# One tile for the output projection's two PSUM banks, evicted by one VectorE product, and one more convolution tap on TensorE in eleven warm-up steps

## The chip, the cores and the metric

One core of a Trainium2 chip, one launch, all data in float32. The metric is the device time of one launch in microseconds (us). The engines are TensorE (PE in the profile, with PEld for its weight loads), VectorE (DVE), ScalarE (ACT), GpSimd (POOL) and SyncE (SP, which here only issues DMAs). Matmuls write into PSUM, which has eight banks of 128 partitions by 512 float32; everything else lies in SBUF.

## The reference, cut to what matters

```python
# x: (2, 768, 64, 64).  d_inner 1536, 4 states per channel, 12 heads of 64
x = x + layer0(group_norm(x))
x = x + layer1(group_norm(x))

def layer0(h):                        # selective scan over 4096 positions per image
    x  = h @ in_proj_w.T              # 768 -> 1536 channels
    xs = silu(depthwise_conv3x3(x) + conv_b)
    dt, Bs, Cs = split(xs @ x_proj_w.T, [48, 4, 4])
    delta = softplus(dt @ dt_w.T + dt_b)
    s[t]  = exp(delta * A) * s[t-1] + (delta * xs) * Bs      # 4 states per channel
    y     = sum_over_states(s * Cs) + D * xs
    y     = layer_norm(y) * ln_g + ln_b                      # over the 1536 channels
    return y @ out_proj_w.T           # 1536 -> 768 channels

def layer1(h):                        # attention by channel statistics
    w   = h @ W_qkv.T                 # 768 -> 768
    Pi  = softmax over the heads of sum_d (w / |w|_over_positions)**2 * temp
    dots = sum over positions of Pi_n * w**2
    return -(w * Pi / (1 + dots)) @ W_out.T
```

## The kernel before, in words

**Layer 0** is a pipeline of 192 steps (NQ0): 16 tiles of 512 positions (NI, 8 image rows each, TL = 512), times 12 chunks of 128 channels (KI). The main loop calls `step(g)` for one (tile, chunk) after the other; the order of all instructions in it is written out by hand (`tc.manual_schedule()`), so every engine works its queue in the order of the code. In step g the scan of chunk g runs. Work for later and earlier chunks lies beside it:

- the input projection of chunk n = g + 17 (`in_proj`, matmul L375), whose result ScalarE copies into a padded image `xs`;
- the convolution taps of chunk a = g + AHEAD = g + 15. Nine taps are split: the middle one is ScalarE's (`tap_act`, L438); those in DMA_TAPS are scaled by ScalarE (`taps_act`, L450) and added by accumulating DMAs; those in PE_TAPS are matmuls with a diagonal matrix into the accumulator's bank (`taps_pe`, L477, the diagonal written by ScalarE in `diag`, L432); what is left, three to five, are VectorE's (`taps_dve`, L491), one instruction each. The tables repeat every four chunks;
- for chunk g: POOL's du = delta * u (`du`, L548), VectorE's product with B (`scan`, L567), the scan (L570) and the product with C (`times_c`, L577); POOL's `sum1` (L556) and accumulating DMAs form y; ScalarE's `square` (L587) and TensorE's `sums_pair` (L597) the layer norm's sums;
- the output projection of a tile runs 12 steps behind (BEHIND): in each step `out_proj` (L636) accumulates three chunks into two banks, for two of the six output chunks, kk by kk, bank 0 then bank 1. Every fourth step these two are full.

After the four steps `out_evict` (L650) multiplies the two banks by the row `rs` (the inverse deviation of the layer norm) into two SBUF buffers. It is called in steps g = 16, 20, ..., 204: from `taps_dve`, after the first of VectorE's taps; from step 177 on, where there are no taps any more, at that place in the step, but for 180, 184 and 188, where it comes in the scan of the step before, after L567 (`early`). Then `out_residual` (L658, an accumulating DMA on POOL's queue) adds x, `out_sums` (L672, two steps after the evict) takes the next group norm's sums on ScalarE, and `out_store` (L680, SP's queue) writes the two to DRAM.

SBUF buffers of 512 columns come from one FIFO of N_SLOT slots: `take()` takes the oldest free one, `give()` returns one.

**PSUM**: psA, psC, psX, psS hold one bank each, psZ one tile of two banks, psO two tiles of one bank each, tags po0 and po1. The users of psO are: the output projection (po0 and po1); odd chunks of the input projection in the first steps, and the lower rows of the first tile (po1); Strassen's w (po0) and x (po1) in the second layer; and two of the six tiles in `spread` (ppo). One output group of the last tile uses psZ instead (poz).

**Layer 1** does its two projections mostly in Strassen's form with seven products (`strassen`, matmul L921), each of three matmuls of 256 columns. (The trace counts two instructions for each matmul of the code, here and elsewhere: a product shows as six, often as a row of x4 and one of x2.) A block q of kind "p1" (the first projection) or "p3" (the second, which adds the residual) goes: t1 into w[:, lo], b21 into x[:, lo], ScalarE's copy of w into p5 (L1003), t2 into y, VectorE's addition of y and p5 into x[:, hi] (L1010), the next block's b11 into another bank y2, eviction of x[:, lo] (`evict`: VectorE L946 and ScalarE's squares L947 for p1, one VectorE addition for p3), t3 into y. Then, in a p1 block only, VectorE adds y and p5 (L1019) and ScalarE squares that sum for its accumulated total, with w[:, lo] as the place for the squares, which nobody reads (L1020). Then b22 into x[:, hi], t4 into y, the eviction of x[:, hi], ScalarE's copy of y2 into the next x (L962), and the eviction of y. In the profile the tiles of all blocks appear as po_p (w and x), psa_p and acc_p (y). There are 30 blocks of p1 with L1020 in the page's counts and 42 of p3.

Of the kernel before, what the change touches and what calls it, by code (L numbers as in the profile page):

```python
# [7 lines left out]
F32 = mybir.dt.float32  # L8
# [6 lines left out]
P = 128  # L15
# [7 lines left out]
KI = DI // P  # L23
# [8 lines left out]
TL = TR * W  # L32
NT = H // TR
NI = NB * NT
NQ0 = NI * KI
# [12 lines left out]

DMA_TAPS = ((0, 2, 6), (0, 2, 6), (0, 2, 6), (0, 2))
PE_TAPS = ((), (1,), (), (1, 7))  # L50
FILL_TAPS = ((0, 2), (0, 2, 6))
NA = 5 * W

AHEAD = 15
BEHIND = 12

N_SLOT = AHEAD + BEHIND + 9 + 9 + 1
N_WEIGHT = 4
N_MORE = 33

# [8 lines left out]
def both_layers(  # L69
# [5 lines left out]
    wp = ctx.enter_context(tc.tile_pool(name="l0w", bufs=1))  # L75
# [29 lines left out]
    rs = wp.tile([P, TL], F32, name="rs")  # L105

    slots = [wp.tile([P, TL], F32, name=f"u{j}") for j in range(N_SLOT)]

    def take():
        return slots.pop(0)  # L110

    give = slots.append
# [7 lines left out]
    def give_w(w):  # L120
        wst.append(w.rearrange("p k m -> p (k m)"))
# [5 lines left out]
    psO = ctx.enter_context(tc.tile_pool(name="l0_pso", bufs=1, space=PSUM))  # L127
    psS = ctx.enter_context(tc.tile_pool(name="l0_pss", bufs=1, space=PSUM))


    spare = psC.tile([P, 512], F32, tag="acc", name="acc_spare")

# [179 lines left out]
    xts, wis, wos, pas, accs, dgs, pxs, pzs, sts, pos, xrs = {}, {}, {}, {}, {}, {}, {}, {}, {}, {}, {}  # L312

    def where(n):
        i, c = divmod(n, KI)
        return i, c, i // NT, i % NT
# [43 lines left out]
    def in_proj(n):  # L360
        i, c, b, t = where(n)
        nn = TL if t < NT - 1 or b + 1 < NB else TL - W
        w = wis.pop(n)
        if KI <= n < AHEAD + 2 and n % 2:
            pa = psO.tile([P, 512], F32, tag="po1", name=f"pa{n}")
        else:
            pa = psA.tile([P, 512], F32, tag="psa", name=f"pa{n}")
        parts = [(pa, slice(0, nn))]
        if i == 0:
            pl = psO.tile([P, 512], F32, tag="po1", name=f"pl{n}")  # L370
            parts = [(pa, slice(0, NA)), (pl, slice(NA, TL + W))]
            pas["low", n] = pl
        for o, cols in parts:
            for k in range(KM):
                nc.tensor.matmul(  # L375
                    o[:, : cols.stop - cols.start], w[:, k, :], xts[i, k][:, cols], start=(k == 0), stop=(k == KM - 1)
                )
        pas[n] = pa
        give_w(w)
        if c == KI - 1:  # L380
            for k in range(KM):
                xt = xts.pop((i, k))
                if i:
                    give(xt)
# [23 lines left out]
    def dma_taps(a):  # L408
        return DMA_TAPS[a % 4] if a >= AHEAD else FILL_TAPS[a < 8] if a != KI - 1 else ()

    def pe_taps(a):
        return PE_TAPS[a % 4] if a > AHEAD else ()

# [206 lines left out]
    def out_proj(g, behind_first=lambda: None):  # L622
        i, r = (g - BEHIND) // KI, g % KI
        w = wos.pop(g)
        give_w(w)
        if r % 4 == 0:
            if i == NI - 1 and r == 4:
                pz = psZ.tile([P, 2, 512], F32, tag="pz", name=f"poz_{g}")
                pos[0] = [pz[:, e, :] for e in range(2)]
            else:  # L630
                pos[0] = [psO.tile([P, 512], F32, tag=f"po{e}", name=f"po{e}_{g}") for e in range(2)]
        po = pos[0]
        for kk in range(3):
            k = 3 * (r % 4) + kk
            for e in range(2):
                nc.tensor.matmul(  # L636
                    po[e], w[:, kk, e * P : (e + 1) * P], us[i * KI + k], start=(k == 0), stop=(k == KI - 1)
                )
            if r // 4 == 2:
                give(us.pop(i * KI + k))  # L640
            if kk == 0:
                behind_first()

    def out_evict(g):

        po = pos[0]
        i, r = (g - 1 - BEHIND) // KI, (g - 1) % KI
        for e in range(2):
            xr = take()
            nc.vector.tensor_mul(xr, po[e], rs)  # L650
            xrs[i, 2 * (r // 4) + e] = xr

    def out_residual(g):
# [20 lines left out]
    def out_store(g):  # L674
        i, r = (g - 3 - BEHIND) // KI, (g - 3) % KI
        b, t = divmod(i, NT)
        for e in range(2):
            m = 2 * (r // 4) + e
            xr = xrs.pop((i, m))
            nc.sync.dma_start(x1[b][m * P : (m + 1) * P, t * TL : (t + 1) * TL], xr)  # L680
            give(xr)


    scale1 = [gp.tile([P, KM], F32, name=f"scale1_{b}") for b in range(NB)]
# [4 lines left out]
    x1s, w1s, pis, pits, ats, dots, phs = {}, {}, {}, {}, {}, {}, {}  # L689
# [202 lines left out]
    def strassen(todo, last=(), beside=lambda q, place: None, then=()):  # L892
# [9 lines left out]
        have, xr, at = {}, {}, {"load": 0, "use": 0}  # L902
# [30 lines left out]
        def load_res(q):  # L933
            if q < len(blocks) and blocks[q][0] == "p3":
                _, b, j, m = blocks[q]
                for r in range(2):
                    xr[q, r] = load_xr1(b, j, m + KH * r)
# [14 lines left out]
        def bank(pool, tag, q):  # L952
            return pool.tile([P, 512], F32, tag=tag, name=f"{tag}_{'_'.join(map(str, blocks[q]))}")

        def first(q):
            y = bank(*((psA, "psa"), (psC, "acc"))[q % 2], q)
            times(y[:, lo], "b11", start=True)
            return y

        def copy(q, y):  # L960
            x = bank(psO, "po1", q)
            nc.scalar.copy(x[:, lo], y[:, lo])  # L962
            return x

# [22 lines left out]
        def some_jobs(q):  # L987
            run(scalar_jobs, 2)
            run(pool_jobs, 4 if q % KH == 2 else 2)

        def products():
            y = first(0)
            x = copy(0, y)
            stores = []
            for q, (kind, b, j, m) in enumerate(blocks):
                load_res(q + 1)
                jobs_of(q)
                beside(q, 0)
                w = bank(psO, "po0", q)
                times(w[:, lo], "t1", start=True)  # L1000
                times(x[:, lo], "b21")
                p5 = wk.tile([P, TL], F32, tag="sq", name=f"p5_{'_'.join(map(str, blocks[q]))}", bufs=3)[:, lo]
                nc.scalar.copy(p5, w[:, lo])  # L1003
                if kind == "p3":
                    nc.gpsimd.tensor_add(xr[q, 1][:, hi], p5, xr[q, 1][:, hi])
                some_jobs(q)
                beside(q, 1)
                times(y[:, lo], "t2")
                run(stores)
                nc.vector.tensor_add(x[:, hi], y[:, lo], p5)  # L1010
                y2 = first(q + 1) if q + 1 < len(blocks) else None
                evict(q, x[:, lo], 0, 0)
                beside(q, 2)
                some_jobs(q)
                times(y[:, lo], "t3")
                if kind == "p1":
                    w1s[b, m + KH, j] = take()
                    c22 = w1s[b, m + KH, j][:, hi]
                    nc.vector.tensor_add(c22, y[:, lo], p5)  # L1019
                    nc.scalar.activation(  # L1020
                        w[:, lo], c22, AF.Square, accum_out=ss[b][:, m + KH, 2 * j + 1 : 2 * j + 2]
                    )
                else:
                    evict(q, y[:, lo], 1, 1)
                times(x[:, hi], "b22")
                times(y[:, lo], "t4")
                if m == KH - 1:
                    tile_done(kind, b, j)
                evict(q, x[:, hi], 0, 1)
                if y2 is not None:  # L1030
                    x = copy(q + 1, y2)
                some_jobs(q)
                evict(q, y[:, lo], 1, 0)
                if kind == "p3":
                    stores = [
                        (lambda d, v: lambda: store_out(*d, v))((b, j, m + KH * r), xr.pop((q, r))) for r in range(2)
                    ]
                y = y2
            run(scalar_jobs)
            run(stores)  # L1040
# [70 lines left out]
    def spread(b, j, ms):  # L1111

        for m in ms:
            if m in (0, 4):
                pits["z"] = psZ.tile([P, 2, 512], F32, tag="pz", name=f"ppz{b}_{j}_{m}")
            if m == 2:
                pits["o"] = [psO.tile([P, 512], F32, tag=f"po{e}", name=f"ppo{e}_{b}_{j}") for e in range(2)]
            pb = pits["o"][m % 2] if m in (2, 3) else pits["z"][:, m % 2, :]
            r = 32 * (m % 4)
            nc.tensor.matmul(pb, esel[r : r + HEADS, m, :], pits[b, j][r : r + HEADS, :], start=True, stop=True)  # L1120
            pits[b, j, m] = pb
# [565 lines left out]
```

## Time and profile before

| | |
|---|---|
| median of 3 runs (lowest to highest) | 3651.55 us (3648.76 to 3654.29) |
| the profiled run, its span | 3651.83 us, 3650.0 us |
| granted TensorE clock, mean | 0.991 |
| PE busy, PEld | 3533.1 us (97%), 1785.9 us (49%) |
| DVE, ACT, POOL busy | 2811.2 us (77%), 2573.5 us (71%), 1796.1 us (49%) |
| L636 output projection | 2256 matmuls, 1001.6 us busy |
| L570 scan | 192, 851.1 us, 4433 ns each |
| L491 VectorE taps | 690, 520.0 us, 754 ns each |
| window 170 to 325 us | PE 115.63 of 155.00, DVE 147.90, ACT 128.93, clock 0.86 |
| window 325 to 2450 us | PE 2105.89 of 2125.00, DVE 2053.52, ACT 1892.87, clock 1.00 |
| window 3150 to 3314 us (p1 blocks) | PE 163.40 of 164.00, DVE 38.80, ACT 76.72, clock 1.00 |

A row of a timeline gives the start in us from the begin of the span, the time taken, the engine and line, the operation, tile written <- tiles read with their shapes, xN where N instructions are drawn as one row, and in brackets the idle time of the engine before the row and what ended it. ACTIVATION_READ_ACCUMULATOR is the reading out of ScalarE's running sum. The granted clock says how fast TensorE was let run, 1.00 being full speed.

### The profile page before, as it was taken

The page shows a single profiled execution, that of the slowest core. Times are in us where ns is not written, and L with a number is a line of the kernel's source. Part 1 is how long each engine was busy: PE and PEld are TensorE (multiplying, and loading weights), DVE is VectorE, ACT ScalarE, POOL GpSimd, SP SyncE. Part 2 cuts the span into 40 slices and gives each one's busy share as a digit, 9 for nine tenths or more (in the row PEclk, how much of TensorE's full clock was granted, in tenths as well). Part 3 has the DMA queues.
Part 4 walks back from the last instruction along what each step waited for, and adds up shares of the span by engine and source line. Part 5 has one row for each costly group of instructions (what it writes and reads, how often), then busy time and mean ns, then how long its engine had stood idle before and what let it go on. Part 6 is the DMA issues. An engine that isn't in the chain of part 4 may idle for free. (4 is left out here: it accounts for less than half of the span.)

```text
span 3650.0 us, 37942 instructions
## 1 busy us (share of the span) xinstructions
PE 3533.1 (97%) x11202; PEld 1785.9 (49%) x11202; DVE 2811.2 (77%) x2528; ACT 2573.5 (71%) x5028; POOL 1796.1 (49%) x1808
## 2 busy tenths in 40 slices
PE   6879999999999999999999999999999999999999
PEld 4423444444434444344344444433347658885688
DVE  8899999999999999999999999996722352225522
ACT  2788988988899898988889898886633532244221
POOL 2555656565655666665556665653444213330242
PEclk9989999999999999999999999999999999999999
DMA  9668899998989989899888989986566538863587
GB/s 350 207 133 178 179 215 204 202 210 189 209 185 217 206 192 208 188 214 205 183 197 190 210 189 217 207 188 162 144 199 209 172 109 268 262 204 119 168 268 241
DMA packets 374333, 729.79 MB, mean 200 GB/s; under 512 B 42912, under 2 KB 115200, under 8 KB 370032
## 3 DMA queue, kind: packets, MB, share of 16 engines
q0 software_dynamic: 142176, 262.73, 41.8%
q1 hardware_dynamic: 231952, 464.64, 38.7%
q8 instruction: 90, 1.47, 0.2%
q14 instruction: 115, 0.94, 0.1%
HBM read 439.11 MB, written 60.03 MB: 137 GB/s over the span
## 5 line engine op out<-in xcount | busy, mean ns | idle before, releaser
L636 PE MATMUL po<-u,w 128*128 128x512 f32 x2256 | 1001.6, 592 | 1.8 <-DVE u L650 1.8
L375 PE MATMUL pa<-u,w 128*128 128x512 f32 (+1 forms) x2160 | 966.7, 597 | 1.6 <-ACT carry L400 1.6
L570 DVE TENSOR_TENSOR_SCAN s<-da,s 128x2052 f32<-128x2052 f32 x192 | 851.1, 4433 | 21.0 <-DVE s L567 1.4
L636 PEld LDWEIGHTS po<-u,w 128*128 128x128 f32 x2256 | 428.1, 190 | 539.3 <-issue 528.0
L375 PEld LDWEIGHTS pa<-u,w 128*128 128x128 f32 x2160 | 406.3, 192 | 555.0 <-issue 534.8
L556 POOL TENSOR_TENSOR ysum<-da 128x1024 f32<-128x1024 f32 x192 | 386.2, 2011 | 556.5 <-DVE da L577 486.0
L491 DVE SCALAR_TENSOR_TENSOR acc<-xs,pc,acc 128x512 f32<-128x512 f32 x690 | 520.0, 754 | 27.5 <-ACT acc L438 6.1
L567 DVE TENSOR_TENSOR s<-du,bc 128x2048 f32<-128x2048 f32 x192 | 439.2, 2288 | 81.7 <-POOL du L548 79.5
L456 POOL DMA_DIRECT2D tm<-tm x309 | 268.7, 870 | 455.2 <-ACT tm L450 397.2
L544 ACT ACTIVATE da<-dl,neg_a 128x512 f32<-128x512 f32 x768 | 489.6, 713 | 0.0
L577 DVE TENSOR_TENSOR da<-s,bc 128x2048 f32<-128x2048 f32 x192 | 440.0, 2292 | 6.3
L563 POOL DMA_DIRECT2D u<-ysum x384 | 379.6, 1254 | 3.0 <-issue 1.9
L450 ACT ACTIVATE tm<-xs,pc 128x512 f32<-128x512 f32 x486 | 317.1, 717 | 10.2 <-DMA tm<-tm 5.1
L438 ACT ACTIVATE acc<-xs,pc 128x512 f32<-128x512 f32 x192 | 131.6, 686 | 211.0 <-DVE u L491 200.8
L548 POOL TENSOR_TENSOR du<-dl,u 128x512 f32<-128x512 f32 x192 | 245.2, 1277 | 0.0
L460 POOL DMA_DIRECT2D u<-tm x177 | 209.6, 1184 | 38.0 <-DMA tm<-tm 13.0
L921 PE MATMUL po_p<-u,w 128*128 128x256 f32 x684 | 177.6, 379 | 0.1
L597 PE MATMUL st<-sq,ones 128*32 128x512 f32 x384 | 130.0, 625 | 37.2 <-ACT sq L587 37.0
L921 PE MATMUL po_p<-v,w 128*128 128x256 f32 x612 | 160.2, 379 | 1.5 <-ACT po_p L1020 1.4
L491 DVE SCALAR_TENSOR_TENSOR u<-xs,pc,acc 128x512 f32<-128x512 f32 x192 | 143.6, 748 | 8.3
L477 PE MATMUL acc<-xs,dg 128*128 128x512 f32 x264 | 135.3, 622 | 11.5 <-ACT acc L438 11.4
L560 ACT ACTIVATE u<-u,pc 128x512 f32<-128x512 f32 x192 | 136.7, 712 | 7.1 <-POOL du L548 7.1
(291 smaller groups left out, 5001.5 us busy)
## 6 DMA issues: line engine op xcount, KB each, us to landing
u<-ysum POOLq DMA_DIRECT2D x384, 256.0 KB, 5.9
tm<-tm POOLq DMA_DIRECT2D x309, 256.0 KB, 4.7
w<-in_wP SPq DMA_DIRECT2D x192, 384.0 KB, 4.1
w<-wo_dr SPq DMA_DIRECT2D x192, 384.0 KB, 4.8
u<-x SPq DMA_DIRECT2D x277, 256.0 KB, 4.4
w<-s_dr_p SPq DMA_DIRECT2D x288, 192.0 KB, 2.9
u<-tm POOLq DMA_DIRECT2D x177, 256.0 KB, 6.2
bc<-bc_dr SPq DMA_DIRECT2D x32, 1024.0 KB, 7.9
```

The lines of the kernel that those rows point to most:

```text
L375: nc.tensor.matmul(o[:, : cols.stop - cols.start], w[:, k, :], xts[i, k][:, cols], start=(k == 0), stop=(k == KM - 1))
L450: nc.scalar.activation(tm.rearrange("p (h w) -> p h w", w=W), xs[:, dy : dy + TR, dx : dx + W], AF.Copy, scale=pc[:, c, PC_W + j : PC_W + ...
L456: nc.gpsimd.dma_start(tms[a][0], tms[a][q], accum_op=ALU.add)
L491: nc.vector.scalar_tensor_tensor(dst, xs[:, dy : dy + TR, dx : dx + W], pc[:, c, PC_W + j : PC_W + j + 1], acc, ALU.mult, ALU.add)
L544: nc.scalar.activation(das[g % 2][:, n, 1:], deltas[g], AF.Exp, scale=neg_a[:, c, n : n + 1])
L556: nc.gpsimd.tensor_add(ysum[:, 0 : 2 + g % 2 : 1 + g % 2, :], da[:, 0:2, 1:], da[:, 2:4, 1:])
L563: nc.gpsimd.dma_start(us[g], ysums(g, n), accum_op=ALU.add)
L567: nc.vector.tensor_mul(s[:, :, 1:], dus.pop(g).unsqueeze(1).to_broadcast([P, NS, TL]), bc[:, :NS, :])
L570: nc.vector.tensor_tensor_scan(sf, das[g % 2].rearrange("p n l -> p (n l)"), sf, 0.0, ALU.mult, ALU.add)
L577: nc.vector.tensor_mul(das[g % 2][:, :, 1:], s[:, :, 1:], bc[:, NS:, :])
L636: nc.tensor.matmul(po[e], w[:, kk, e * P : (e + 1) * P], us[i * KI + k], start=(k == 0), stop=(k == KI - 1))
L921: nc.tensor.matmul(dst, half[:, k, :], tiles[blocks[seq[i][0]][:3]][what][k], start=(start and k == 0), stop=(k == KH - 1), skip_group_che ...
```

## The change

Three things. psO holds one tile `po_both` of two banks, made once, and all users of po0 and po1 take its halves by `po_bank(0)` and `po_bank(1)`. In the 41 evictions of steps 16 to 176 (`paired`), one VectorE product of 128x2x512 writes a fixed buffer `xr_both` of two chunks; the residual DMAs, sums and stores work on its halves, and the halves go to the slots with the last such store; in exchange N_SLOT is two less. The other seven evictions stay two products into slots. WARM_TAPS gives tap 1 to TensorE in the even chunks a = 16 to 26 too, which are prepared by steps g = 0 to 10 and would be VectorE's in steps 1 to 11.

```diff
+WARM_TAPS = ((1,), (1,), (1,), (1, 7))
-N_SLOT = AHEAD + BEHIND + 9 + 9 + 1
+N_SLOT = AHEAD + BEHIND + 9 + 9 - 1
...
+    po_both = psO.tile([P, 2, 512], F32, tag="po", name="po")
+    xr_both = wp.tile([P, 2, TL], F32, name="xr")
+
+    def po_bank(e):
+        return po_both[:, e, :]
...
 def in_proj(n):
-            pa = psO.tile([P, 512], F32, tag="po1", name=f"pa{n}")
+            pa = po_bank(1)
...
-            pl = psO.tile([P, 512], F32, tag="po1", name=f"pl{n}")
+            pl = po_bank(1)
...
 def pe_taps(a):
-        return PE_TAPS[a % 4] if a > AHEAD else ()
+        return (PE_TAPS if a > AHEAD + KI else WARM_TAPS)[a % 4] if a > AHEAD else ()
...
 def out_proj(g, ...):
-                pos[0] = [psO.tile([P, 512], F32, tag=f"po{e}", name=f"po{e}_{g}") for e in range(2)]
+                pos[0] = [po_bank(e) for e in range(2)]
...
+    def paired(g):
+        return g < NQ0 - AHEAD
+
     def out_evict(g):
         po = pos[0]
         i, r = (g - 1 - BEHIND) // KI, (g - 1) % KI
+        if paired(g):
+            nc.vector.tensor_mul(xr_both, po_both, rs.unsqueeze(1).to_broadcast([P, 2, TL]))
         for e in range(2):
-            xr = take()
-            nc.vector.tensor_mul(xr, po[e], rs)
+            if paired(g):
+                xr = xr_both[:, e, :]
+            else:
+                xr = take()
+                nc.vector.tensor_mul(xr, po[e], rs)
             xrs[i, 2 * (r // 4) + e] = xr
...
 def out_store(g):
-            give(xr)
+            if not paired(g - 2) or not paired(g + 2):
+                give(xr)
...
 def copy(q, y):
-            x = bank(psO, "po1", q)
+            x = po_bank(1)
...
 def products():
-                w = bank(psO, "po0", q)
+                w = po_bank(0)
...
 def spread(b, j, ms):
-                pits["o"] = [psO.tile([P, 512], F32, tag=f"po{e}", name=f"ppo{e}_{b}_{j}") for e in range(2)]
+                pits["o"] = [po_bank(e) for e in range(2)]
```

## The prediction

> **What bounds the kernel now.** I read the page first, then VectorE's timeline in the front and in the steady stretch, then the timelines of all engines around three uses of the banks that the change joins.
>
> ```profile
> PE 3533.1 (97%) x11202; PEld 1785.9 (49%) x11202; DVE 2811.2 (77%) x2528; ACT 2573.5 (71%) x5028; POOL 1796.1 (49%) x1808
> ```
>
> TensorE is the bound over the whole, and in the second layer it is the only one: the windows give it 163.40 busy us of 164.00 in 3150 to 3314, where VectorE has 38.80. From 170 to 325 it is otherwise: TensorE 115.63 of 155.00 at a granted clock of 0.86, VectorE 147.90. From 325 to 2450 both are near the end, 2105.89 and 2053.52 of 2125.00. VectorE's timeline in the front:
>
> ```profile
> 222.75 4.43 DVE L570 TENSOR_TENSOR_SCAN s<-da,s 128x2052 f32<-128x2052 f32 x1
> ...
> 235.64 4.43 DVE L570 TENSOR_TENSOR_SCAN s<-da,s 128x2052 f32<-128x2052 f32 x1
> ...
> 245.75 2.29 DVE L567 TENSOR_TENSOR s<-du,bc 128x2048 f32<-128x2048 f32 x1 [0.32 <-POOL du L548]
> 248.14 4.43 DVE L570 TENSOR_TENSOR_SCAN s<-da,s 128x2052 f32<-128x2052 f32 x1
> ```
>
> Scan to scan, the step with five VectorE taps takes 12.89 us, the next with four 12.50. The four-tap step has a wait of 0.32 for POOL's du that the five-tap step hides. So a tap less is worth 0.39 there, not its 0.78 (four took 3.12). The output eviction in the steady stretch, VectorE's timeline:
>
> ```profile
> 629.68 1.28 DVE L650 TENSOR_TENSOR u<-po,rs 128x512 f32<-128x512 f32 x2
> 630.88 1.54 DVE L491 SCALAR_TENSOR_TENSOR acc<-xs,pc,acc 128x512 f32<-128x512 f32 x2
> ```
>
> Two products hold VectorE for 1.20 us, start to next start. Now all engines near the end of layer 0, where the products wait for the matmuls. First with po0 and po1 as two tiles:
>
> ```profile
> 2493.62 4.46 PE L636 MATMUL po<-u,w 128*128 128x512 f32 x10
> ...
> 2497.26 0.69 DVE L650 TENSOR_TENSOR u<-po,rs 128x512 f32<-128x512 f32 x1 [2.25 <-PE po L636]
> ...
> 2498.12 0.69 DVE L650 TENSOR_TENSOR u<-po,rs 128x512 f32<-128x512 f32 x1 [0.17 <-PE po L636]
> ```
>
> The first product starts 0.82 before the last matmul ends (2493.62 + 4.46 = 2498.08): it waited for its own bank only. Then a step whose banks are one tile of two (poz, out of psZ):
>
> ```profile
> 2734.55 3.17 PE L636 MATMUL poz<-u,w 128*128 128x512 f32 x7
> ...
> 2737.75 1.29 DVE L650 TENSOR_TENSOR v<-poz,rs 128x512 f32<-128x512 f32 x2 [30.21 <-PE poz L636]
> ```
>
> The matmuls, in the same order of banks, end at 2737.72, and both products start after that, back to back. **A tile of two banks is waited for as a whole.** That is the row on which my forecast turns, because the change puts the Strassen tiles w (po0) and x (po1) into one tile as well. A "p1" block on the timeline:
>
> ```profile
> 3212.32 1.03 PE L921 MATMUL po_p<-u,w 128*128 128x256 f32 x4
> ...
> 3213.04 0.39 ACT L1020 ACTIVATE po_p<-u 128x256 f32<-128x256 f32 x1 [1.64 <-DVE u L1019]
> ...
> 3213.36 0.19 ACT L1020 ACTIVATION_READ_ACCUMULATOR po_p<-u 128x1 f32 x1
> ...
> 3214.85 0.36 ACT L962 COPY po_p<-acc_p 128x256 f32<-128x256 f32 x1
> 3214.91 1.03 PE L921 MATMUL po_p<-u,w 128*128 128x256 f32 x4
> ```
>
> The first row is b22 into x; L1020 writes its unused squares into w, which is then free; L962 copies into the next x while t1, the last row, goes into the next w. Today none of these meets another's bank.
>
> **The change part by part.** All sums stand against the profiled run, 3651.83 (span 3650.0), 0.28 above the median of 3651.55.
>
> *One more TensorE tap in steps 1 to 11.* Six VectorE taps go, at odd steps. The scan periods of steps 1 to 12 alternate 12.89 and 12.50, but for step 2, whose 2.44 wait for POOL's du swallows what step 1 saves: 5 x 0.39 = **-1.95** (six would give -2.3, none 0). Added: 12 tap matmuls (L477) at a pitch of 0.43, 5.2 us in the 39.4 that TensorE idles in that window, and six diag writes on ScalarE (L432), 0.4 each, in its 26.1 idle. Both at nothing; with the cover gone, +5.2 and +2.4.
>
> *One product for two.* 41 evictions (steps 16 to 176). The product of 512 takes 0.684, the one of 2048 (L567) 2.288; on the line between them 1024 elements take 1.22 and hold VectorE some 1.13 instead of 1.20: 0.066 saved, times 41 = 2.7. Twelve steps take VectorE 154.35 and TensorE 154.0, so two thirds are taken: **-1.8**, between 0 and -2.7.
>
> *One fixed buffer in place of two slots.* The product now waits until the stores of the eviction before have read xr_both; behind it VectorE would hold taps and the scan. The first store is issued at 399.4 after the evict at 371.2, stores land within 3.2 to 6.0, and the next evict is at 422.72: at least 13.5 us to spare, so **0**; the residual DMAs on POOL's queue go out some 6 us after the product as before. A store that took all of that and more would cost its excess in each of 40 steps. Slots: two fewer in the pool, two fewer in use; the least reserve stays two. **0**.
>
> *The shared tile in layer 0.* A step's next output matmuls wait for both products rather than one; they follow the eviction by some 2 us nearly everywhere. At 2348.37 and 2665 the margin is nil: **+1.1** for both.
>
> *The shared tile in the 30 p1 blocks* (L1020: 16 + 14). b22 comes after L1020 in program order and now writes the same tile, so it waits for its end: 3213.36 + 0.19 = 3213.55, and 0.05 to pass it on, against a start of 3212.32: 1.28 (mean of the blocks 1.30). 30 x 1.30 = **+39.0**. Below, if the accumulator's read need not be waited for, 3213.43 + 0.05 - 3212.32 = 1.16, or 34.8. Then t1 waits for L962: 3215.21 + 0.05 - 3214.91 = 0.35, in the 25 blocks that a p1 block follows in the same call **+8.8**; at the first blocks of two calls 0.61 each **+1.2**. After a stall the first matmul takes longer: at 2779.463 the pitch was 0.32 where 0.216 is usual, 0.10 x 57 stalls = **+5.7**. Nothing else is late there to hide it: VectorE and ScalarE are idle over half of that stretch, and every row after b22 moves with it. In the 42 p3 blocks there is no L1020, and the copy ends 0.28 before t1: 0.
>
> Does TensorE's clock bear stalls of 1.3 us? The trace has both: after one of 1.32 at 407.72 the window 404 to 412 stands at 1.00; after one of 1.82 at 1028.49 the window 1028 to 1032 stands at 0.57, and the next 12 matmuls of L375 took 6.25 for 5.31 to 5.42 elsewhere. I take 0, as 1.30 is nearer to the first; a drop costs some 1.8 with its ends, and one in three blocks would make +18.
>
> The Trainium skill ("TensorE: Matmul & The Clock Gate", section "Why this matters for your kernels") warns only of TensorE gaps above some 3 us; by it no stall here would cost clock, which the row at 1028.49 contradicts. The same skill ("PSUM — Partial Sum Buffer", section "PSUM bank collisions raise a hardware error") asks for guards by bank and partition quadrant; guarded so, b22 in one bank would not wait for L1020 in the other, the +55.8 would be nothing and the time 3647.8, but the poz row shows that this program's waits go by the tile.
>
> Sum: 39.0 + 8.8 + 1.2 + 5.7 + 1.1 = 55.8; with -1.95 and -1.8, +52.05. From the median, **3703.6**.
>
> **The rivals.**
> *The banks stay separate* (the poz wait came from the order of its matmuls, or holds for reads only): only -3.75 remains, 3647.8, within the 0.2% (7.3 us) that a measurement of this kernel can tell from no change. For it speaks that matmul and ScalarE touch different banks; against it poz.
> *Faster: the banks stay separate, and VectorE's earlier finish also ends TensorE's waits* in 325 to 2450, 19.1 us idle, most of them before L597 for ScalarE's sq (L587), which follows VectorE's chain. It decides once over 2.7 of those 19.1 go; with half gone and the whole 2.7 of the evictions: -1.95 - 2.7 - 9.5, 3637.4. Against it: ScalarE itself is busy 1892.87 of 2125, and 0.2 us in 12 steps moves its start little.
> *The clock falls in the torn p1 stretch*: +18, 3721.6. For it the 0.57 window, and 0.86 in the front, where TensorE is often idle.
>
> **How the numbers follow.** Forecast 0.77, clock 0.07, banks separate 0.10, faster 0.06. So slower 0.84, same 0.10, faster 0.06. Low end: 34.8 alone, with -2.3 and -2.7: 3681. High end: the forecast with +18, 5.2 and 2.4: 3729. The two cases below the range hold 0.16.
>
> **What would show it.** L650 as 41 products of 128x1024 at about 1.22; the odd steps of the front at 12.50; in p1 blocks an idle of 1.3 before b22 that ScalarE ends and 0.35 before t1; a p1 block of 10.9 us instead of 9.07, p3 blocks unchanged; 3150 to 3314 longer by some 33, the first p1 stretch (2757 to 2873) by some 20. I am wrong if p1 blocks keep 9.07, if the products wait for a store, or if PEclk drops in the second layer.

## The result, and the profile after

| | before | after |
|---|---|---|
| median (lowest to highest), 5 runs each | 3649.80 us (3648.76 to 3654.29) | 3712.64 us (3710.95 to 3715.60) |
| ratio, 95% interval | | 1.0168 (1.0157 to 1.0179) |
| span of the profiled run | 3650.0 us | 3711.4 us |

The change costs 62.8 us by the medians, 61.4 by the spans of the two profiled runs; 52 were forecast. Line numbers shift by 7 in layer 0's taps and scan, and by 16 in the second layer: L921 is now L937, L1020 is L1036, L962 is L978. The page's totals:

```profile
PE 3553.9 (96%) x11214; PEld 1785.5 (48%) x11214; DVE 2804.8 (76%) x2481; ACT 2576.7 (69%) x5034; POOL 1795.9 (48%) x1808
```

VectorE has 6.4 us less work in 47 fewer instructions, TensorE 12 instructions more, so the change does what it says. The paired eviction, a row of the groups by line with shapes kept apart (busy us, mean ns, idle before):

```profile
L659 DVE TENSOR_TENSOR xr<-po,rs 128x1024 f32<-128x1024 f32 x41 | 49.9, 1217 | 0.0
```

It takes the 1.22 us of the interpolation, 41 times, and no idle time stands before it: the fixed buffer is never waited for. In the front, VectorE's timeline:

```profile
222.84 4.43 DVE L577 TENSOR_TENSOR_SCAN s<-da,s 128x2052 f32<-128x2052 f32 x1
...
232.94 2.29 DVE L574 TENSOR_TENSOR s<-du,bc 128x2048 f32<-128x2048 f32 x1 [0.31 <-POOL du L555]
235.34 4.43 DVE L577 TENSOR_TENSOR_SCAN s<-da,s 128x2052 f32<-128x2052 f32 x1
...
245.44 2.29 DVE L574 TENSOR_TENSOR s<-du,bc 128x2048 f32<-128x2048 f32 x1 [0.31 <-POOL du L555]
247.84 4.43 DVE L577 TENSOR_TENSOR_SCAN s<-da,s 128x2052 f32<-128x2052 f32 x1
```

Both periods are 12.50 now; the first was 12.89. The wait for POOL's du, hidden in that step before, has come out (0.31), as the working said: 0.39 of a tap's 0.78 is gained. A p1 block, timeline of all engines:

```profile
3262.03 0.39 ACT L1036 ACTIVATE po<-u 128x256 f32<-128x256 f32 x1 [0.17 <-DVE u L1035]
3262.36 0.19 ACT L1036 ACTIVATION_READ_ACCUMULATOR po<-u 128x1 f32 x1
...
3262.60 0.70 PE L937 MATMUL po<-u,w 128*128 128x256 f32 x2 [1.12 <-ACT po L1036]
...
3265.23 0.36 ACT L978 COPY po<-psa_p 128x256 f32<-128x256 f32 x1
...
3265.64 1.13 PE L937 MATMUL po<-u,w 128*128 128x256 f32 x4 [0.18 <-ACT po L978]
```

Read the brackets: b22, which writes the second bank, now starts 0.05 after ScalarE has written unused squares into the first bank and read out its sum (3262.36 + 0.19); t1, which writes the first bank, starts 0.05 after a copy into the second. The trace counts the idle from the modelled end of the matmul before; by starts, b22 comes 1.496 after its predecessor instead of 0.216, so it is 1.28 late.

Where the 61.3 us between the last events of the two traces went, by the same events in both, each the growth of a stretch:

| stretch | before | after | growth |
|---|---|---|---|
| up to the first scan | 169.85 | 170.39 | +0.5 |
| scan 1 to scan 12 | 142.47 | 140.46 | -2.0 |
| scan 12 to the output projection of step 18 | 86.72 | 87.48 | +0.8 |
| from there to that of step 174 | 2027.23 | 2024.58 | -2.7 |
| from there to the first Strassen block | 331.88 | 336.76 | +4.9 |
| the 12 p1 blocks of the first call | 116.27 | 140.87 | +24.6 |
| the second call, 18 p1 and 18 p3 blocks | 327.94 | 362.29 | +34.3 |
| the third call, 24 p3 blocks, and what lies between | 443.94 | 444.79 | +0.8 |

### The profile page after: what moved, and what is told of

Same layout as the page of the kernel before. It is cut to its first block, busy times and chain, and to the rows that moved or that the text cites. A ratio compares the mean times of both kernels' runs of the same rounds, so it can differ in the third digit from the quotient of the medians.

```text
span 3711.4 us, 37951 instructions
## 1 busy us (share of the span) xinstructions
PE 3553.9 (96%) x11214; PEld 1785.5 (48%) x11214; DVE 2804.8 (76%) x2481; ACT 2576.7 (69%) x5034; POOL 1795.9 (48%) x1808
## 5 line engine op out<-in xcount | busy, mean ns | idle before, releaser
L382 PE MATMUL pa<-u,w 128*128 128x512 f32 (+1 forms) x2136 | 949.9, 594 | 1.1 <-ACT carry L407 1.1
L574 DVE TENSOR_TENSOR s<-du,bc 128x2048 f32<-128x2048 f32 x192 | 439.3, 2288 | 85.3 <-POOL du L555 81.5
L937 PE MATMUL po<-v,w 128*128 128x256 f32 x612 | 164.3, 387 | 25.9 <-ACT po L1036 23.3
L937 PE MATMUL po<-u,w 128*128 128x256 f32 x612 | 164.5, 384 | 17.6 <-ACT po L1036 13.7
L484 PE MATMUL acc<-xs,dg 128*128 128x512 f32 x276 | 144.4, 632 | 18.7 <-ACT acc L445 18.7
L1019 ACT COPY p_p<-po 128x256 f32<-128x256 f32 x72 | 26.8, 372 | 168.0 <-PE po L937 168.0
```

Of the source, the lines that this page charges most:

```text
L382: nc.tensor.matmul(o[:, : cols.stop - cols.start], w[:, k, :], xts[i, k][:, cols], start=(k == 0), stop=(k == KM - 1))
L574: nc.vector.tensor_mul(s[:, :, 1:], dus.pop(g).unsqueeze(1).to_broadcast([P, NS, TL]), bc[:, :NS, :])
L937: nc.tensor.matmul(dst, half[:, k, :], tiles[blocks[seq[i][0]][:3]][what][k], start=(start and k == 0), stop=(k == KH - 1), skip_group_che ...
```

## The experiments

The theories: (A) the joint tile is waited for as a whole, so that b22 and t1 wait for ScalarE's work in the other bank; (B) the loss comes from the fixed buffer or the wide product; (C) the banks are waited for apart, and something else stretches the blocks. Two numbers of each trace are used: the TensorE time of the two calls with p1 blocks (444.2 before, 503.2 after), and the time from step 174's output projection to the second layer ("late", 331.88 and 336.76). Each trace is one execution and not the median one: e3's and e5's are the fastest run of theirs, e6's is the second slowest.

**e1, w apart.**

```diff
-                w = po_bank(0)
+                w = bank(psX, "px", q)
```

> The changed kernel with one line more: Strassen's w is taken from psX's bank, which is idle in these stretches, so that w and x are two tiles again; pairing, fixed buffer and taps stay. If the 62.8 us come from waits on the tile as a whole (A), b22 and t1 no longer wait and the p1 blocks go back to 9.07 us from 10.98: the 59.0 us that TensorE lost in the two p1 stretches come back, 3654, less the 2.7 of the clock drop there if that is counted apart. If the loss lies in layer 0 or in the fixed buffer (B), it stays near 3712. If the banks are waited for apart and something else stretches the p1 blocks (C), no change either.

3650.51 us against 3651.98 of the kernel before, ratio 0.9995 (0.9987 to 1.0004). The calls take 115.40 and 328.08: the p1 blocks are as they were. This excludes (B), as everything else of the change was still in it.

**e2, the squares into SBUF.**

```diff
-                        w[:, lo], c22, AF.Square, accum_out=...
+                        junk, c22, AF.Square, accum_out=...      # junk: a tile of the pool wk, tag "sq"
```

> The changed kernel with the unused squares of L1036 written into an SBUF buffer instead of w. Under (A) only the wait of b22 goes, 30 times 1.28 + 0.10 and some 5 more in the one block where ScalarE's queue was long, and the wait of t1 for the copy into x stays (0.35 + 0.10 in 25 to 27 blocks): about 3713 - 42 - 5 = 3666, a p1 block of 9.5 us. Under (B) and (C) 3712.

3665.30 us, ratio 1.0041 (1.0029 to 1.0053). Groups by line, busy us, mean ns, and the idle before them with its releasers; first the matmuls into the joint tile in the changed kernel:

```profile
L937 PE MATMUL po<-u,w 128*128 128x256 f32 x612 | 164.5, 384 | 17.6 <-ACT po L1036 13.7 <-ACT po L978 2.2 <-issue 1.2
L937 PE MATMUL po<-v,w 128*128 128x256 f32 x612 | 164.3, 387 | 25.9 <-ACT po L1036 23.3 <-issue 1.1 <-ACT po L978 1.0
```

and in e2:

```profile
L937 PE MATMUL po<-u,w 128*128 128x256 f32 x612 | 163.2, 382 | 3.8 <-ACT po L978 2.0 <-issue 1.2 <-POOL v L882 0.5
L937 PE MATMUL po<-v,w 128*128 128x256 f32 x612 | 161.0, 381 | 4.8 <-ACT po L978 3.2 <-issue 1.1 <-POOL v L882 0.5
```

The 37.0 us behind L1036 are gone and the waits behind the copy L978 stay, so the two terms come apart: from its t1 to the next block's t1, a p1 block of the second call takes 9.07 us before, 9.52 in e2 (+0.45, t1's wait and restart) and 10.92 after (+1.40 more, b22's; medians). Over both calls e2 lies 14.3 above before, and the changed kernel 44.7 above e2.

**e3, the joint tile alone.** The kernel before with `po_both` and `po_bank`, two products into slots as before, no WARM_TAPS.

> The kernel before with the joint tile alone: no pairing (two products into slots, as before), no extra taps. Under (A) nearly the whole loss is there without the two other parts: 3650 + 59 + 3 for the later waits in layer 0, about 3712 to 3716, a p1 block of 10.98. Under (B), which needs the fixed buffer or the wide product, about 3650.

3718.81 us, ratio 1.0178 (1.0164 to 1.0192): the loss is there without pairing and taps, 3 us above the 3712 to 3716 expected. The calls take 139.70 and 362.13 in its trace. (A) holds; (B) is excluded a second time.

**e4, one bank evicted.** e1 with the product cut to `xr_both[:, 0, :]`, and the buffer set to zero once at the start.

> e1 with the paired product cut to its first bank: the second half of the buffer is not written (its outputs are not the reference's), which takes 41 x some 0.53 = 22 us off VectorE. It asks what a shorter eviction can be worth in steps 16 to 176. If TensorE sets the pace there, as the offsets of its matmuls after the change suggest (they gain about 0.3 us where VectorE was relieved of 2.7), the time falls by under 5 us against e1; if VectorE sets it, as my -1.8 assumed for two thirds, by some 15 us.

3640.79 us, 9.7 below e1. 22 us less on VectorE in steps 16 to 176 are worth 9 to 10: between the two expectations. By the traces, step 18 to step 174 shrank by 9.2 against e1. So a microsecond taken off VectorE there is worth 0.42 on average: it sets the pace in a part of the steps only.

**e5, taps alone**, **e6, pairing alone** and **e7, both**, the last two with the joint tile closed before the output projection of step 176 and two one-bank tiles in the same PSUM space after it:

```diff
+    joint = ExitStack()
+    psP = joint.enter_context(tc.tile_pool(name="l0_psp", bufs=1, space=PSUM))     # po_both is made here
+    apart = []
+    def po_apart(e, name):
+        if not apart:
+            joint.close()
+            apart.append(ctx.enter_context(tc.tile_pool(name="l0_pso", bufs=1, space=PSUM)))
+        return apart[0].tile([P, 512], F32, tag=f"po{e}", name=name)
...
-                pos[0] = [po_bank(e) for e in range(2)]
+                pos[0] = [po_bank(e) if paired(g + 1) else po_apart(e, f"po{e}_{g}") for e in range(2)]
...
-                w = po_bank(0)          # and x and the ppo tiles likewise
+                w = po_apart(0, ...)
```

> The kernel before with WARM_TAPS alone. By my sum scans 1 to 12 come 1.95 to 2.35 us closer together than before (142.47 us from the first to the twelfth) and the rest is unchanged: 3648 to 3650, no difference that this measurement can tell. A rival: TensorE, taken from its idle time, also reaches the steady stretch earlier and loses it there, so that nothing is left at the end of layer 0.

> The paired eviction alone, with the joint tile closed before the output projection of step 176 and two tiles of one bank after that, as before; no extra taps. If the pairing is worth its 41 x 0.066 on VectorE and no more, the output projection of step 174 starts 0 to 2.7 us earlier against step 18 than before; if the joint tile costs something in the steady stretch too (the second bank's matmuls wait for the whole product), it shows here as a start that is later. From step 174 to the second layer the time is 331.88 as before, not 337 as in all four kernels with the joint tile. 3647 to 3651.

> The whole change, pairing and taps, with the joint tile closed before step 176: the version that the first four runs point to. If the joint tile is all that loses, in the late steps (5 us from step 174 to the second layer) and in Strassen's p1 blocks (59 us), what is left are the gains: -2 from the taps and up to -2.7 from the pairing, 3645 to 3648 against 3650 to 3652 of the kernel before, and some 4 under e1. If the late loss comes from stalls and clock drops that any earlier VectorE brings, it stays at e1's 3650.5.

e5: 3652.63 us, ratio 0.9999 (0.9990 to 1.0008). e6: 3652.80, 1.0003 (0.9994 to 1.0012). Neither is a gain that can be seen, and both lie above the times expected, as the kernel before does in these runs (3652.80). e7: **3648.19, ratio 0.9988 (0.9980 to 0.9997)** against 3652.80 of the kernel before on the same chip, so 4.6 us faster by the medians, 1.1 to 7.3 by the interval. How the 4.6 divide is open: alone, the two parts come to -0.2 and 0.0.

The same two banks, as two tiles again, have no wait in the p1 blocks but the one that the kernel before has too. (They are the same: of PSUM's eight banks the other pools hold six.) Groups by line, first before, then e7:

```profile
L921 PE MATMUL po_p<-v,w 128*128 128x256 f32 x612 | 160.2, 379 | 1.5 <-ACT po_p L1020 1.4
```

```profile
L945 PE MATMUL po_p<-u,w 128*128 128x256 f32 x612 | 161.6, 379 | 0.0
L945 PE MATMUL po_p<-v,w 128*128 128x256 f32 x612 | 160.2, 380 | 1.4 <-ACT po_p L1044 1.4
```

This is what excludes (C): not the banks but the tile decides. Late, e6 and e7 take 334.4 and 333.9, where the kernels whose joint tile lives on take 335.2 (e4) to 337.6 (e8). The forecast for e6 and e7 of 331.88 late was missed by 2.0 to 2.5; all but 0.5 to 0.8 of that is a clock drop at 174 (below).

The rival to e5's gain is not excluded. In e5's trace scan 1 to 12 shrank by 3.1 and the second layer starts 3.7 earlier, but some 1.7 of the 3.7 are a clock drop of the kernel before, at 1028.49, which e5 did not have, and the median shows no gain. Over all traces the first to the twelfth scan took 139.37 to 140.46 with the taps (after, e1, e2, e4, e5, e7; mean 140.0) and 141.61 to 142.47 without (before, e3, e6, e8; mean 142.0): -2.1, without overlap. Step 18 to step 174 took 2022 to 2027 with the pairing (after, e1, e2, e6, e7) and 2025 to 2027 without (before, e3, e5, e8): means 2023.8 and 2025.9, a difference of 2.1, in a scatter that is larger: after and e1, the same code there, differ by 2.8, and e6 gained only 0.1 (it lost clock at 1032.53, as the kernel before did at 1028.49).

**e8, the joint tile in layer 0 alone**: e3 with w apart.

> The joint tile in layer 0 alone: no pairing, no taps, Strassen's w apart. It prices the shared tile in layer 0, which my prediction put at +1.1: by the trace of e3, which has the same layer 0, +3 to +5, so 3653 to 3657; by my prediction 3651 to 3653.

3656.38 us, ratio 1.0008 (0.9999 to 1.0017), +3.6 by the medians, which the interval does not tell from nothing; its late stretch takes 337.56, 5.7 more than before. The timeline of the changed kernel at the first of the unpaired evictions shows what the tile does there; to be read beside the row pair of 2497.26 and 2498.12 that the prediction shows:

```profile
2491.09 5.31 PE L643 MATMUL po<-u,w 128*128 128x512 f32 x12
...
2496.44 1.29 DVE L665 TENSOR_TENSOR u<-po,rs 128x512 f32<-128x512 f32 x2 [4.59 <-PE po L643]
2497.64 4.42 DVE L577 TENSOR_TENSOR_SCAN s<-da,s 128x2052 f32<-128x2052 f32 x1
```

Both products now lie behind the last matmul (2496.40): the scan starts 1.24 after it where it was 0.64 (2498.72 after 2498.08). These evictions (`early`, steps 180, 184 and 188) sit between the product L574 and the scan, and the squares that TensorE's sums wait for follow VectorE's chain. What that costs is seen from the output projection of step 181 to the second layer: in the six kernels whose joint tile lives on this stretch is 2.5 (after, e2) to 5.2 us (e1) longer than before, 3.2 in e8; in e5, e6 and e7 it is the same within 0.02. TensorE's wait for sq before step 187's output projection shows it, before and after:

```profile
2594.93 1.58 PE L597 MATMUL st<-sq,ones 128*32 128x512 f32 x2 [2.77 <-ACT sq L587]
```

```profile
2594.57 1.88 PE L604 MATMUL st<-sq,ones 128*32 128x512 f32 x2 [3.43 <-ACT sq L594]
```

This wait is 0.66 longer in all six, and 2.77 in e5, e6 and e7 as before. The next, before step 191's, is 1.75 or 1.76 without the joint tile and 2.38 to 2.75 with it. The rest is clock that was lost after the two waits, and 0.6 at the output projection of step 192 in e3, e4 and e8. Up to step 181 the kernels do not differ by the tile: from step 174 the changed kernel has lost 2.3 there, but e6 and e7, with the tile closed, 2.5 and 2.0, and e1, with it, nothing.

## Why the prediction was right, and where its terms were off

The time lies in the range, 9 us above the forecast value, and the mechanism is the one forecast: its rivals "banks separate" and "faster" fell with the brackets behind L1036 and L978 and with e3 and e7. Of the 9 us, 4 are in the p1 calls, 4 late in layer 0, and the rest in growths of under 1 us that the forecast did not have. Term by term:

- **b22 behind L1036**: 1.30 + 0.10 in each block was right (1.40 between e2 and after), and so was the sign, a p1 block of 10.9 instead of 9.07 (10.92). What was not seen is one block of the first call. I took 1.30 as the mean and passed over a block in which ScalarE's queue is long. Timeline of the changed kernel:

```profile
2779.47 0.42 DVE L1035 TENSOR_TENSOR v<-acc_p,p_p 128x256 f32<-128x256 f32 x1 [1.68 <-PE acc_p L937]
...
2782.88 0.36 ACT L1036 ACTIVATE po<-v 128x256 f32<-128x256 f32 x1
...
2783.43 2.93 PE L937 MATMUL po<-v,w 128*128 128x256 f32 x6 [4.05 <-ACT po L1036]
```

  The data are there at 2779.9, but ScalarE first works off layer 0's last sums (L687) and two normalisations (L731), and b22 waits 4.05 us and TensorE's clock falls: it is granted 0.50 from 2783 to 2789, and the matmuls there come 0.427 apart instead of 0.216, some 2.8 more in all. Before, only the end of that queue was felt (1.40 at 2779.46). The block took 15.15 for 9.38. The block makes up most of what separates the 59.0 measured in the two calls from the 54.7 of the p1 terms.
- **t1 behind the copy L978**: 0.35 and 0.10 were right; 14.3 measured in e2 in all for the 12.7 of the sum, since the wait stands in more blocks than the 25 and two (in all of the second call's p1 blocks).
- **The clock**: taken as 0, rival at 0.07. Right for the stalls of 1.3 us, none of which lost it; of the 30 blocks the one with the stall of 4.05 did. In layer 0 two waits for sq that the kernel before has as well were as long or one us longer after and lost 1.7 each; rows of before and after, TensorE's timeline:

```profile
2436.19 1.04 PE L597 MATMUL st<-sq,ones 128*32 128x512 f32 x2 [2.56 <-ACT sq L587]
2437.17 5.42 PE L727 MATMUL pq<-u,w 128*128 128x512 f32 x12
```

```profile
2432.82 1.04 PE L604 MATMUL st<-sq,ones 128*32 128x512 f32 x2 [2.54 <-ACT sq L594]
2433.79 7.11 PE L743 MATMUL pq<-u,w 128*128 128x512 f32 x12
```

  The same wait, 12 matmuls in 5.42 and in 7.11: chance decided here, not the tile (e6 and e7 lost it too, after 2.54 and 2.35; e4 did not, after 2.55). The second, at 2644.64, grew from 1.75 to 2.74, and the 24 matmuls after it took 12.10 for 10.40 by starts.
- **The shared tile in layer 0**: +1.1 forecast, for a longer wait of two output projections. Both are in the traces: at 2348.37 the idle before it went from 1.27 to 1.81, and at 2665 from 0.54 to 1.14 in e3, e4 and e8 (in the changed kernel that step comes so late that nothing is waited for). The step that failed: I priced only the evictions without a margin to the next output projection and passed over the three that sit before a scan, though the prediction shows the first of them as its example. In the changed kernel they made two waits for sq 0.66 and 0.99 longer, and the second lost the clock (1.7); from step 181 on that is 2.5 in all. The other 2.3 of the late +4.9 came before: 1.7 from the drop at 174, and 0.7 at step 181, which e6 and e7 have as well.
- **The taps**: -1.95 forecast, -2.0 in the changed kernel, -2.1 over all traces. (The tap goes to TensorE in six of the eleven warm-up steps that the title names, the odd ones.) **The pairing**: -1.8 forecast; -2.1 over all traces is within their scatter of it, and of nothing. In the profiled pair (-2.7) some 1.7 are a clock drop of the kernel before, at 1028.49, which the changed kernel did not have. By e4's share of 0.42 the two thirds taken were too many: an estimate from it is 1.1 of the 2.7.
- **The fixed buffer and the slots**: 0, right (no idle before L659). **p3 blocks**: 0 forecast, +0.7 in the last call of every kernel whose w and x share the tile.

## What to carry to other kernels

Before two buffers are put into one tile, list everybody who uses either half, in every stage, and ask for each pair whether one now waits for the other: the tile, not the bank, was what the program waited for, and a write of data that nobody reads was the dearest wait. A joint tile may pay where its halves are filled and emptied together, if its life ends there: closed before the stages that use the halves apart, it no longer cost the 59 us, and the kernel was 4.6 us faster than before (1.1 to 7.3 by the interval). When the cost of a new wait is taken from one typical block, look at the longest queue of the releasing engine too: one block of 30 cost as much as three.

## What the runs showed of the hardware that was not expected

The loss of TensorE's clock follows the length of an idle, but not sharply. In the ten traces, take the waits of `sums_pair` for sq after 325 us by the start of the matmul less the start of the one before less 0.43 (some 0.15 above the bracket's number): from 0.97 to 1.93, none of 33 lost the clock; from 1.99 to 2.72, 8 of 16; from 2.90 on, all 23. A loss cost 1.65 to 3.1 us. Of two waits before an output projection, one of 1.98 in e3 lost it (its 12 matmuls took 7.11) and one of 1.99 in e8 did not. The length is not all: at one spread in the second layer all ten traces have a wait of 1.0, and four of them (e1, e4, e6, e7) lost 1.7 us of clock after it. The Trainium skill ("TensorE: Matmul & The Clock Gate", section "Why this matters for your kernels") puts the limit for gaps at about 3 us; by these runs half of the waits of 2.0 to 2.7 us already cost clock. And executions of the same layer 0 differ by up to 2.8 us between step 18 and step 174 (after and e1), so that gains of 2 us are seen, if at all, in the traces of many kernels and hardly in one time.
